# Layer 2 of a graph-attention kernel: both square roots of the norm ahead of the diagonals on ScalarE

## The chip, the cores and the metric

The kernel runs on one core of one Trainium2 chip. A core has five engines with a queue of instructions each: PE (TensorE, matrix products), DVE (VectorE), ACT (ScalarE), POOL (GpSimd, which here only issues gathers and scatters by index) and SP (SyncE, which issues plain DMAs). Each engine takes its own instructions in the order in which they were written, and waits on semaphores for the others. PE records stand in the profile as PE (the passes of a product) and PEld (weight loads). The metric is the device time of one execution in microseconds (us).

## What is computed

Two graph-attention layers on 10000 nodes with 768 features and about 170000 edges, then a residual and a layer norm. Cut to what matters (`gat_conv` is softmax attention over the edges that end in a node):

```python
h = gat_conv(x, edge_index, W1, a_src1, a_dst1, b1, HEADS, HID, True)     # 4 heads of 256
h = relu(layer_norm(h, g1, be1)) + (x @ Wr1 + br1)
h1 = h
h = gat_conv(h, edge_index, W2, a_src2, a_dst2, b2, 1, OUT_DIM, False)    # 1 head of 768
h = layer_norm(h, g2, be2)
h = h + (h1 @ Wr2 + br2)
x = _layernorm(x + h)
```

The change lies in layer 2: the attention sum of a row of table 2 over a node's edges, the norm with g2 and be2, the product of h1 with Wr2, and the last norm.

## The kernel before

A first stage computes table 1 (x times W1, with the attention terms) for all nodes and sorts the nodes by degree. `ordered_layer1` does layer 1 and writes table 2 (rows of 770 numbers) and h1. `ordered_layer2`, the function of this case, goes over 79 tiles of 128 nodes. Nodes of a tile have up to n edges; n is `SLOTS[t]` and grows over the tiles: 8, 9, 10, three of 11, three of 12, five of 13, six of 14, eight of 15, seven of 16, eight of 17, seven each of 18 and 19, six of 20, then four of 21 and so on up to 27, and a last tile of 41.

For edge slot k of a tile, POOL gathers 128 rows of table 2 into one place of a ring of 40 places (L393). The gather for a place waits until both readers of its old row are done. The weighted sum over the slots is split between two engines: DVE does columns 0 to 511 (`weigh`, L476, one instruction a slot, into `acc` in PSUM), PE does columns 512 to 767: ACT writes a diagonal matrix with the weights of slot k (L820), and PE multiplies it with the gathered rows and adds into `sum` (L821, two passes a slot in the records, after two passes of L814 for the bias). There are two buffers of four diagonals, so that the ninth diagonal has to wait until PE is done with the first four. PE also does the residual product of the next tile (L830 and L832, 36 passes).

All order is as written (`manual_schedule`). An iteration t of the loop at L842 does, for the tile before (`last`), the two norms and the store, and for tile t the attention sum:

- `stats = deviation(...)` (L855): DVE takes the statistics of `acc` and `sum` (L518, L520), ACT the square root (L522).
- `next(tail)` (L856): ACT writes the first n // 2 diagonals of tile t, PE multiplies them.
- `scaled` (L857; L531, L533, L534 on DVE), the residual is added (L858), `deviation` of the result (L859): DVE statistics, and the second square root on ACT.
- L861: the rest of the diagonals. L875: the residual product of tile t + 1 on PE.
- the loop over the slots (L888): DVE weighs slot k, POOL gets the gather of the place that this frees. After slot 1 comes `finish()` (L864): a reciprocal of the second square root on DVE (L865), L867, and on ACT the last scaling into `o` (L868). In the last three slots DVE and ACT make the weights of the next tile (`weights_of`: L804, L438 to L446 with an Exp on ACT, then L459 to L456).
- POOL scatters `o` to the output (L905). There is one buffer for `o`, so L868 waits until the scatter of the tile before has landed.

So ACT's order for a tile is: square root 1, diagonals 0 to n // 2 - 1, square root 2, the other diagonals, the last scaling, a table load, the Exp of the next tile, a table load.

Of the kernel before, what the change touches and what calls it, by code (L numbers as in the profile page):

```python
# [46 lines left out]
LEAD = 3  # L47
# [29 lines left out]
def gnn_kernel(ctx, tc, x, x_cols, src, dst, src_col, dst_col, W1, a_src1, a_dst1, b1, g1, be1, Wr1, br1,  # L77
# [7 lines left out]
    NT = -(-N // P)  # L85
# [4 lines left out]
    SLOTS = CAPS  # L90
# [301 lines left out]
    def gather(to, table, index, **more):  # L392
        nc.gpsimd.indirect_dma_start(out=to, out_offset=None, in_=table,  # L393
                                     in_offset=bass.IndirectOffsetOnAxis(ap=index, axis=0), **more)
# [152 lines left out]
    def load(s, w):  # L547
        nc.sync.dma_start(s[:, :, :w.shape[1]], w.rearrange("(k p) n -> p k n", p=P))
# [82 lines left out]
    SLOTS, FIRST = SLOTS[::-1], FIRST[::-1]  # L631
# [140 lines left out]
    def ordered_layer2():  # L772
        nonlocal ps_big
        with tc.tile_pool(name="b2", bufs=1) as pool, tc.tile_pool(name="small2", bufs=2) as small, \
                tc.tile_pool(name="ps_acc2", bufs=2, space=PSUM) as ps_acc, \
                tc.tile_pool(name="ps_q2", bufs=2, space=PSUM) as ps_big, tc.manual_schedule():
            ring = Ring(pool, table2, R2, RING2)
            ring.fetch(SLOTS[0])

            wr2, parts = w2[:, :, :C2], [wr1[:, k, :] for k in range(K0)]  # L780
            load(wr2, Wr2)
            b2_b, g2_b, be2_b = (spread(pool, v, n) for v, n in ((b2, "b2"), (g2, "g2"), (be2, "be2")))
            more = pool.tile([P, C2], F32, name="out")
            nc.scalar.dma_start(more, bass.AP(tensor=br2.tensor, offset=br2.offset, ap=[[0, P], [1, C2]]))
            nc.vector.tensor_add(be2_b, be2_b, more)
            brT = spread_br1(pool, "brT")
            more = pool.tile([P, C2], F32, name="out")
            nc.scalar.dma_start(more, shift.to_broadcast([P, C2]))
            nc.vector.tensor_add(b2_b, b2_b, more)

            def fetch_x(t):

                hT, xt = parts[t % 2], parts[2 + t % 2][:, :D0]
                nc.sync.dma_start(hT, h1_d[t])
                gather(xt, x[:, :], nodes(t))
                return hT.rearrange("p (k n) -> p k n", n=P), xt

            ones = pool.tile([1, P], F32, name="ones")
            nc.vector.memset(ones, 1.0)
            def weights_of(t):  # L800

                n = SLOTS[t]
                ad = small.tile([P, H2], F32, name="ad")
                nc.vector.tensor_add(ad, ring.slot(FIRST[t])[:, C2 + H2:], lift)  # L804
                e, _ = logits(small, ring, FIRST[t], FIRST[t] + n, ad, H2, C2)
                yield e
                normalised(small, e, H2, t)
                yield

            def sums(t, acc, e):  # L810


                n = SLOTS[t]
                nc.tensor.matmul(acc, ones, b2_b[0:1, ON_PE2:], start=True, stop=False)  # L814
                for k in range(n):
                    if k == n // 2:
                        yield
                    if k % G == 0:
                        diagonals = pool.tile([P, G, P], F32, name="diagonals", bufs=2)
                    nc.scalar.activation(diagonals[:, k % G, :], ident, AF.Copy, scale=e[:, k, :])  # L820
                    nc.tensor.matmul(acc, diagonals[:, k % G, :],  # L821
                                     ring.slot(FIRST[t] + k)[:, ON_PE2:C2], start=False, stop=(k == n - 1))

            def residual(t):

                hT, xt = ins.pop(t)
                r = ps_big.tile([P, 2 * BANK], F32, name="big")
                for c in range(0, C2, BANK):
                    d = min(C2, c + BANK)
                    nc.tensor.matmul(r[:, c:d], ident, xt[:, c:d], start=True, stop=False)  # L830
                    for j in range(K1):
                        nc.tensor.matmul(r[:, c:d], hT[:, j, :], wr2[:, j, c:d], start=False,  # L832
                                         stop=(j == K1 - 1))
                return r

            ins = {t: fetch_x(t) for t in range(min(2, NT))}
            ring.fetch(RING2)
            rs = {}
            last = None
            ready = []  # L840
            assert SLOTS[0] <= ring.size and NT > 1
            for t in range(NT + 1):  # L842
                live, tail = t < NT, iter(())
                n = SLOTS[t] if live else 0
                whole = live and n <= ring.size
                if whole and not ready:
                    ready = list(weights_of(t))
                if whole:
                    e = ready[0]
                    acc = ps_acc.tile([P, BANK], F32, name="acc")  # L850
                    sum_ = ps_acc.tile([P, BANK], F32, name="sum")[:, :C2 - ON_PE2]
                    tail = sums(t, sum_, e)
                if last:
                    h, r, means = last
                    stats = deviation(small, [a for m in means for a in pieces(m, C2 - ON_PE2)])  # L855
                    next(tail, None)  # L856
                    scaled(h, means, stats, g2_b, be2_b)  # L857
                    nc.vector.tensor_add(h, h, r[:, :C2])  # L858
                    mean, inv = deviation(small, pieces(h, C2 // 2))  # L859
                    o = pool.tile([P, C2], F32, name="out")  # L860
                for _ in tail:  # L861
                    pass

                def finish():  # L864
                    nc.vector.reciprocal(inv, inv)  # L865
                    less = small.tile([P, 1], F32, name="less")
                    nc.vector.scalar_tensor_tensor(less, mean, -1.0, inv, op0=OP.mult, op1=OP.mult)  # L867
                    nc.scalar.activation(o, h, AF.Identity, bias=less, scale=inv)  # L868

                if live:  # L870
                    if not t:
                        rs[0] = residual(0)
                        q = product(brT, wr2, C2)
                    elif t + 1 < NT:
                        rs[t + 1] = residual(t + 1)  # L875
                    r = rs.pop(t)
                    h_ = parts[4 + t % 2][:, :C2]
                    if not whole:
                        if last:
                            finish()  # L880
                        ad = small.tile([P, H2], F32, name="ad")
                        nc.vector.tensor_add(ad, ring.slot(FIRST[t])[:, C2 + H2:], lift)
                        attend_parts(small, ring, h_, h_, ad, b2_b, H2, DH2, t)
                    ready = []
                    ahead = iter(())
                    if whole and t + 1 < NT and SLOTS[t + 1] + LEAD <= ring.size:
                        ahead = weights_of(t + 1)
                    for k in range(n if whole else 0):  # L888
                        if k >= n - LEAD:
                            ready += itertools.islice(ahead, 1)  # L890
                        weigh(acc, ring.slot(FIRST[t] + k), e[:, k], ON_PE2, None if k else b2_b)
                        ring.fetch(FIRST[t] + k + 1 + ring.size)
                        if last and k == 1:
                            finish()
                        if not t and k == n - LEAD:
                            nc.vector.tensor_add(be2_b, be2_b, q[:, :C2])
                            rs[1] = residual(1)
                        if t + 2 < NT and k == n // 2:
                            ins[t + 2] = fetch_x(t + 2)
                    if t + 2 < NT and t + 2 not in ins:  # L900
                        ins[t + 2] = fetch_x(t + 2)
                elif last:
                    finish()
                if last:
                    nc.gpsimd.indirect_dma_start(  # L905
                        out=out, out_offset=bass.IndirectOffsetOnAxis(ap=nodes(t - 1), axis=0),
                        in_=o, in_offset=None, bounds_check=N - 1, oob_is_err=False)
                last = (h_, r, [acc, sum_] if whole else [h_]) if live else None
# [270 lines left out]
```

## Time and profile before

| | |
|---|---|
| median of 3 runs | 6021.35 us (6007.93 to 6030.65) |
| profiled execution | 6084.94 us; span of its instructions 6083.1 us |
| busy in the span | PE 4832.0 us, DVE 4447.5, ACT 3142.5, POOL 3401.9 |
| mean granted clock of PE | 0.890 |
| layer 2, first read of a finished `sum` to the end | 3751 to 6077 us |
| L820 diagonals on ACT | 1336 of 388 ns |
| L821 passes on PE | 2672 of 447 ns (they overlap) |
| L476 in layer 2, 512 columns, on DVE | 1258 of 755 ns |
| L868 last scaling on ACT | 78 of 1013 ns |
| L393 gathers of ring rows in layer 2, on POOL | 1356 of 965 ns |
| table loads on ACT in layer 2 | 77 before the square root, 77 before the Exp, 1283 ns each |

"Busy" is the time in which an engine executes; an engine that waits for a semaphore is idle. In the timeline, a line has the start, the length, the engine, the line of the program, what is written and read, the shapes, how many instructions the line merges, and in brackets the idle time of the engine before it with the engine that ended it ("issue" and "remote": the profile names none). PE's times are those of taking up a pass; its end is modelled.

### The profile page before, as it was taken

What the parts mean: (1) busy time and instruction counts of PE and PEld (TensorE: products, weight loads), DVE (VectorE), ACT (ScalarE), POOL (GpSimd) and SP (SyncE); (2) the same over time, 40 slices, a digit from 0 to 9 for tenths busy, and PEclk for the clock granted to TensorE, in tenths of its full rate; (3) what the DMA queues carried; (4) which work ended last, traced back from release to release, by engine and by line L of the source; (5) the groups of instructions that cost most, each with busy time, mean ns of one, the idle gap of its engine ahead of it and who ended that gap; (6) DMA issues with size and microseconds to landing.
All of it is one profiled execution on the core that took longest, in us unless ns stands there. A gap on an engine that the chain in (4) does not pass through costs nothing. (4 is left out here: it accounts for less than half of the span.)

```text
span 6083.1 us, 56565 instructions
## 1 busy us (share of the span) xinstructions
PE 4832.0 (79%) x14464; PEld 2808.5 (46%) x14464; DVE 4447.5 (73%) x7872; ACT 3142.5 (52%) x8061; POOL 3401.9 (56%) x3396
## 2 busy tenths in 40 slices
PE   8998896999999988888766546988877777777763
PEld 3443343555555554444433323555554555444442
DVE  5872433788999999999988883877666666666667
ACT  3433333678878888788877661333333333333321
POOL 3426444455556666556655525666666666666663
PEclk9999998999999999999888767999888888888876
DMA  4322326789999999999988847888887788887884
GB/s 141 121 86 67 88 87 214 271 297 321 331 327 326 339 340 331 329 324 335 332 314 316 296 166 256 293 292 293 287 269 261 264 277 280 278 281 267 273 272 152
DMA packets 438658, 1580.90 MB, mean 260 GB/s; under 512 B 102763, under 2 KB 106923, under 8 KB 438326
## 3 DMA queue, kind: packets, MB, share of 16 engines
q0 software_dynamic: 341344, 1400.80, 66.4%
q1 hardware_dynamic: 93168, 170.98, 8.5%
q10 hardware_dynamic: 3814, 5.39, 0.3%
q8 instruction: 122, 2.00, 0.1%
q14 instruction: 210, 1.72, 0.1%
HBM read 1431.10 MB, written 146.19 MB: 259 GB/s over the span
## 5 line engine op out<-in xcount | busy, mean ns | idle before, releaser
L393 POOL DMA_INDIRECT ring<-table,slots x2754 | 2622.5, 952 | 1826.0 <-issue 491.9
L476 DVE SCALAR_TENSOR_TENSOR acc<-ring,e,acc 128x256 f32<-128x256 f32 (+1 forms) x2606 | 1609.2, 618 | 189.7 <-PE acc L670 50.6
L465 ACT ACTIVATE ring<-ring,e 128x256 f32<-128x256 f32 x3536 | 1437.0, 505 | 0.0
L472 DVE TENSOR_TENSOR acc<-acc,ring 128x1024 f32<-128x1024 f32 x884 | 1089.1, 1232 | 85.7 <-ACT ring L465 9.4
L832 PE MATMUL big<-w,wr 128*128 128x512 f32 (+1 forms) x2528 | 878.7, 493 | 180.9 <-issue 177.8
L821 PE MATMUL sum<-ring,diagonals 128*128 128x256 f32 x2672 | 774.2, 447 | 258.4 <-issue 228.5
L161 PE MATMUL big<-w,xT 128*128 128x512 f32 x1896 | 834.6, 601 | 59.8 <-DMA xT<-in_x_cols_dram 38.0
L161 PE MATMUL big<-wr,xT 128*128 128x512 f32 x1896 | 866.2, 615 | 17.6 <-ACT xT L543 17.6
L820 ACT ACTIVATE diagonals<-ident,e 128x128 f32<-128x128 f32 x1336 | 424.0, 388 | 846.5 <-PE sum L821 668.7
L161 PE MATMUL big<-w,hT 128*128 128x512 f32 (+1 forms) x2528 | 833.3, 487 | 1.2 <-ACT hT L543 1.2
L821 PEld LDWEIGHTS sum<-ring,diagonals 128*128 128x128 f32 x2672 | 597.2, 227 | 451.2 <-issue 333.9
L832 PEld LDWEIGHTS big<-w,wr 128*128 128x128 f32 x2528 | 484.5, 192 | 527.0 <-issue 495.4
L161 PEld LDWEIGHTS big<-w,hT 128*128 128x128 f32 x2528 | 478.8, 189 | 376.0 <-issue 341.4
L161 PEld LDWEIGHTS big<-w,xT 128*128 128x128 f32 x1896 | 363.5, 193 | 527.5 <-issue 503.0
L161 PEld LDWEIGHTS big<-wr,xT 128*128 128x128 f32 x1896 | 370.6, 199 | 458.3 <-issue 440.5
L670 PE MATMUL acc<-ring,diagonals 128*128 128x256 f32 x1248 | 336.0, 430 | 284.4 <-ACT diagonals L665 251.8
L670 PEld LDWEIGHTS acc<-ring,diagonals 128*128 128x128 f32 x1248 | 269.5, 219 | 345.3 <-ACT diagonals L665 266.2
L618 DVE TENSOR_TENSOR scr<-big,as_b 128x1024 f32<-128x1024 f32 x79 | 96.7, 1224 | 451.8 <-ACT row L615 428.9
L623 POOL TENSOR_TENSOR row<-row,none 128x1024 f32<-128x1024 f32 x79 | 187.0, 2367 | 341.9 <-ACT row L615 341.3
L522 ACT ACTIVATE sd<-mv,eps 128x1 f32<-128x1 f32 x237 | 69.2, 292 | 576.6 <-issue 253.0
L446 ACT ACT_TABLE_LOAD x155 | 198.9, 1283 | 315.6 <-DVE e L445 226.5
L621 ACT ACTIVATE scr<-scr 128x256 f32<-128x256 f32 x632 | 253.5, 402 | 122.2 <-DVE scr L618 117.0
(171 smaller groups left out, 3973.3 us busy)
## 6 DMA issues: line engine op xcount, KB each, us to landing
ring<-table,slots POOLq DMA_INDIRECT x2754
table<-row SPq DMA_DIRECT2D x79, 516.0 KB
h_d<-hT SPq DMA_DIRECT2D x79, 512.0 KB
wr<-h_d SPq DMA_DIRECT2D x79, 512.0 KB
xT<-in_x_cols_dram SPq DMA_DIRECT2D x79, 384.0 KB
w<-in_W_dram SPq DMA_DIRECT2D x6, 512.0 KB
w<-in_W_dram SPq DMA_DIRECT2D x1, 3072.0 KB
wr<-in_Wr_dram SPq DMA_DIRECT2D x1, 3072.0 KB
```

The source lines that it names most:

```text
L161: nc.tensor.matmul(p[:, c:e], aT[:, j, :], w[:, j, c:e], start=(j == 0), stop=(j == k - 1))
L393: nc.gpsimd.indirect_dma_start(out=to, out_offset=None, in_=table, in_offset=bass.IndirectOffsetOnAxis(ap=index, axis=0), **more)
L446: nc.scalar.activation(e, e, AF.Exp)
L465: nc.scalar.activation(row[:, s], row[:, s], AF.Copy, scale=e[:, h:h + 1])
L472: nc.vector.tensor_add(acc[:, :c], acc[:, :c], row[:, :c])
L476: nc.vector.scalar_tensor_tensor(acc[:, s], row[:, s], e[:, h:h + 1], (acc if first is None else first)[:, s], op0=OP.mult, op1=OP.add)
L621: nc.scalar.activation(m[:, s], m[:, s], AF.Copy, accum_out=row[:, C1 + i * H1 + h:C1 + i * H1 + h + 1])
L623: nc.gpsimd.tensor_add(row[:, :C1], row[:, :C1], b1_b)
L670: nc.tensor.matmul(acc[:, c:d], diagonals[:, k * H1 + i, :], ring.slot(FIRST[t] + k)[:, c:d], start=(k == 0 and c % BANK == 0), stop=(k == ...
L820: nc.scalar.activation(diagonals[:, k % G, :], ident, AF.Copy, scale=e[:, k, :])
L821: nc.tensor.matmul(acc, diagonals[:, k % G, :], ring.slot(FIRST[t] + k)[:, ON_PE2:C2], start=False, stop=(k == n - 1))
L832: nc.tensor.matmul(r[:, c:d], hT[:, j, :], wr2[:, j, c:d], start=False, stop=(j == K1 - 1))
```

## The change

Within an iteration, both square roots now come ahead of the diagonals on ACT; the first half of the diagonals follows the second statistics; the second half, and the residual product behind it, follow `finish()` after slot 1.

```diff
-            assert SLOTS[0] <= ring.size and NT > 1
+            assert LEAD <= SLOTS[0] <= ring.size and NT > 1
...
                     stats = deviation(small, [a for m in means for a in pieces(m, C2 - ON_PE2)])
-                    next(tail, None)
                     scaled(h, means, stats, g2_b, be2_b)
                     nc.vector.tensor_add(h, h, r[:, :C2])
                     mean, inv = deviation(small, pieces(h, C2 // 2))
                     o = pool.tile([P, C2], F32, name="out")
-                for _ in tail:
-                    pass
+                    next(tail, None)
+                else:
+                    for _ in tail:
+                        pass
...
                         q = product(brT, wr2, C2)
-                    elif t + 1 < NT:
-                        rs[t + 1] = residual(t + 1)
...
                         if last and k == 1:
                             finish()
+                            for _ in tail:
+                                pass
+                            if t + 1 < NT:
+                                rs[t + 1] = residual(t + 1)
...
+                    if t + 1 < NT and t + 1 not in rs:
+                        rs[t + 1] = residual(t + 1)
```

In the built program the instructions on PE, DVE, POOL and SP stand in the same order as before, one by one; only ACT's order differs. For a tile it is now: square root 1, square root 2, diagonals 0 to n // 2 - 1, the last scaling, the other diagonals, a table load, the Exp of the next tile, a table load.

## The prediction

> **What bounds the kernel now.** I read the waits of layer 2 first (engine, line, what it waited for; total us, times, longest), then the stretches by n, then the timeline of single tiles.
>
> ```profile
> ACT diagonals L820 <- PE sum L821: 668.7, 158, 15.9
> POOL ring L393 <- PE sum L821: 328.2, 200, 8.0
> DVE sd L865 <- ACT sd L522: 146.2, 29, 11.0
> ```
>
> The third line is what the change takes away. The timeline gives it a place: only tiles with n of 18 or more have it. Their first half is nine or more diagonals, the buffers hold eight, so square root 2 stands behind a diagonal that waits for PE. With n up to 17 it comes 5.4 us after DVE's read of the finished `sum`, every time.
>
> Whether these 146 us lie on the path is a matter of what paces a tile. The stretches (PE, PEld, DVE, ACT, POOL busy, clock, DMA share, GB/s) run from one read of `sum` to another, and hold the 8 tiles of n = 15, 8 of 17, 7 of 18 and 7 of 19:
>
> ```profile
> 4151.60:4351.97 200.37, 170.67 (x545) 111.10 (x544) 148.76 (x316) 71.22 (x168) 134.05 (x137) 0.91 0.86 292
> 4557.82:4800.33 242.51, 188.64 (x576) 121.26 (x577) 161.80 (x331) 76.67 (x184) 143.34 (x150) 0.83 0.78 261
> 4800.33:5011.33 211.00, 163.52 (x517) 108.46 (x516) 146.24 (x298) 68.26 (x168) 133.75 (x138) 0.85 0.82 275
> 5011.33:5228.66 217.33, 164.85 (x530) 110.23 (x530) 152.07 (x307) 69.97 (x175) 141.40 (x148) 0.84 0.84 283
> ```
>
> A tile takes 25.05, 30.31, 30.14 and 31.05 us. POOL issues n + 2 transfers a tile (n rows, a row of x, the scatter), one every 1.25 us (0.95 busy, 0.30 to the next), and DMA moves about 315 GB/s while it does. That is 21.25, 23.75, 25.00 and 26.25 us. The rest, 3.8, 6.6, 5.1 and 4.8 us, is mostly a pause of POOL. By the same count n = 14 has 3.4, n = 16 has 6.9, n = 20 has 5.8, and the 15 tiles from 21 to 27 have 6.6 on average. So POOL's issues and one pause a tile make the period. A tile with n = 19:
>
> ```profile
> 5200.61 3.50 PE L821 MATMUL sum<-ring,diagonals 128*128 128x256 f32 x15
> 5207.22 1.02 POOL L905 DMA_INDIRECT out_dram<-out,order  x1 [0.30 <-issue]
> 5211.61 0.40 ACT L820 ACTIVATE diagonals<-ident,e 128x128 f32<-128x128 f32 x1 [10.55 <-remote]
> 5211.72 0.98 POOL L393 DMA_INDIRECT ring<-table,slots  x1 [3.48 <-remote]
> 5211.92 0.28 ACT L522 ACTIVATE sd<-mv,eps 128x1 f32<-128x1 f32 x1
> ```
>
> PE takes up slots 0 to 7 by 5204.1, but ACT and POOL, which both need slot 0 done, go on at 5211.6. In between POOL has stopped for lack of free places; DMA falls from a share of 0.93 (5200 to 5208) to 0.39 (5210.6 to 5211.7), and as it runs dry the waits end. The tiles that I looked at show the same: PE's completions come late while gathers keep DMA full, and together when they stop. Why, the profile doesn't say.
>
> DVE is not in this ring: it sits idle for 7.83 us before 5212.23 and POOL issues at full pace after. PE's sum starts where the residual ends (5200.06), not when a diagonal comes.
>
> **The change part by part.** The order on PE, DVE, POOL and SP stays, so the residual is not moved in PE's own queue; no instruction, table load or DMA is added. Three things move on ACT.
>
> *Square root 2 ahead of the diagonals.* It takes 0.29 us, and DVE's reciprocal no longer waits: minus 146.2 us of DVE idle time. Behind that wait are the weights of slots 2 to n - 1, and behind slot 2 one gather. That costs POOL a second pause in about two thirds of the tiles with n of 18 or more:
>
> ```profile
> 5242.59 0.97 POOL L393 DMA_INDIRECT ring<-table,slots  x1 [4.52 <-PE sum L821]
> 5243.87 0.95 POOL L393 DMA_INDIRECT ring<-table,slots  x1 [0.30 <-issue]
> 5247.59 0.95 POOL L393 DMA_INDIRECT ring<-table,slots  x1 [2.77 <-PE sum L821]
> ```
>
> The third gather needs the place of slot 2. PE is named, but ACT's ninth diagonal shows PE done with slots 0 to 3 by 5244.92, while DVE weighs slot 2 from 5246.10 to 5246.87. I count some 25 such tiles at about 2 us: 50 us of POOL time that go.
>
> What comes instead is read from n = 16 and 17, where the wait does not exist today: there the one pause is 6 to 7 us, the tile 6.9 and 6.6 us over POOL's issues, and DVE waits up to 9.4 us for the end of the sum. With the wait gone, n of 18 and more has the order of n = 17. If the tiles take its 6.7 us, they change by (6.7 - 5.1) x 7 + (6.7 - 4.8) x 7 + (6.7 - 5.8) x 6 + (6.7 - 6.6) x 15 = 31 us slower. If they take the 3.6 of n = 14 and 15: (1.5 + 1.2) x 7 + 2.2 x 6 + 3.0 x 15 = 77 us faster. I take the first, as the nearer row in n and in order of work.
>
> *First half behind square root 2.* Its start moves from 0.9 to 5.7 us after the read of `sum`. PE is then in the residual (36 passes, 11.7 us). In tiles up to 17 the sum starts 7 to 12 us after that read, so the residual covers the delay by 1.5 us or more. From 18 on it starts 2.4 us after the read, but the read itself comes some 4 us earlier once DVE doesn't wait. Cost 0; if that cover fails, up to 4.8 - 1.5 = 3.3 us in 35 tiles, 116 us.
>
> One rule speaks against this part. The Trainium skill (TensorE: Matmul & The Clock Gate, "Part 1: The HAM clock gate") says that after an idle window of about 3.4 us the array runs at half rate. The rows show such phases already: 15 passes in 3.50 us at 5200.61, and 5 in 2.50 us at 5212.07 with a granted clock of 0.50. By the rule a sum that starts late would take twice its passes' time; by the rows, PE works on the residual meanwhile and nothing is added.
>
> *The last scaling ahead of the second half.* It leaves the way of the Exp (1.01 us sooner) and enters the way of the diagonals. In ACT's queue the diagonals, the table load and the Exp stand behind it, and PE's sum and DVE's L459 wait for those. It waits for slot 1's reciprocal, 7 us after the read of `sum`, and for the scatter of the tile before, as `o` has one buffer; today it comes so late that the second wait is 17.1 us in all. The scatter is issued just before POOL's pause. By the DMA shares it lands 3.4 to 4.5 us after its issue. For the tile of n = 13 (read of `sum` at 3900.65) the scatter is issued at 3912.65, lands at 3916.0 to 3917.2, and the scaling ends 1.01 later, at 3917.0 to 3918.2. Diagonals 6 and 7 are written at 3906 today, the eighth and later ones from 3915.71, the Exp at 3919.51. Seven diagonals (2.0 us) and a table load (1.3) behind the scaling put the Exp at 3920.3 to 3921.5, and slots 6 and 7 on PE behind the pause. So 0.8 to 2.0 us later in the 27 tiles with n up to 15, 22 to 54 us, mean 38. POOL's pause may hide it all, and the sum's end moves out by as much as today lies between n = 15 and 16, where the pause doubles. Between 0 and 54 I take 22, a little over half the mean. With n of 16 and 17 the scatter comes 5 to 10 us ahead of the ninth diagonal: 0. From 18 on it is 1.0 us behind that diagonal, in the pause's shadow: 0, at most 35 us.
>
> Sum against the profiled execution: 6084.9 + 31 + 22 = 6138, 0.9% more. It stands 1.06% over the median of the runs; by the same share, 6021 becomes 6074.
>
> **The rivals.**
> *The second pause goes and the first stays short* (faster). For it: the 50 us above, and the 3 us pause that every other tile from 18 on already has. Against it: n = 16 and 17. Price 50 to 77 us, 0.8 to 1.3%: 5944 to 5971. It decides if DVE's earlier read also lets PE take up eight slots before DMA runs dry.
> *Nothing moves.* DMA must run dry once a tile whatever ACT does, and what one pause loses the other gains: 0, give or take 25 us. For it: the time over POOL's issues is 5 to 7 us from n = 16 to 27, with one pause or two. 5996 to 6046.
> *More of the small tiles tip over* (slower still). If n = 14 and 15 go from 3.4 and 3.8 to 6.7: 3.3 x 6 + 2.9 x 8 = 43 us, with the 31: 74 us, 6095; with the 35 us of late diagonals, 6130.
> *That DVE's wait is on the path whole*, minus 146 us, 5875: against it stands POOL, which runs on through that wait.
>
> **How the numbers follow.** 0.5%, 30 us, is about what a measurement of this kernel can tell from no change. Slower, as forecast or with more tiles tipped: 0.52. Nothing moves: 0.24. Faster: 0.24, of which 0.02 below 5940. The likeliest case's own range is 6052 to 6130. Leaving out the ends of both sides, 5955 to 6130 should hold 8 in 10.
>
> **What would show it.** In the profile after, L865's 146 us on L522 must vanish; if it stays, the change does not do what it says. Right: the stretches of n = 18 and 19 at 31.7 and 32.9 us a tile, one POOL pause of 6 to 7 us in each, L868 waiting for the scatter's DMA, the Exp 1 to 2 us later in tiles up to 15. Wrong: stretches of n = 18 and 19 under 29.5 us, or a first `sum` pass of a tile that starts late with ACT as its releaser.

## The result and the profile after

The changed kernel takes 6066.4 us (5 runs, 6061.54 to 6074.03), the kernel before 6025.61 us in the same comparison (5 runs, 6007.93 to 6035.92). The ratio is 1.0071, interval 1.0050 to 1.0091: slower by 0.7%, as forecast in sign; forecast were 6074 us and 0.9%.

One caution comes first. The profiled execution of after took 6074.03 us and is one of these five. That of before took 6084.94 us and lies above all of its five. In a later comparison the same program took 6066 to 6085 us, and in three others 5703 to 5720. So the two profiles may not come from alike chips (for the result no chip is noted): they are compared by stage, not by their totals. And the traces of this level hold fewer semaphore events (updates of a semaphore, with their times), 39286 for before and 42229 for after, than a trace of the same program at 5705 us (74590, the run of before again below). What ended a wait is told from these events, so the names behind the arrows are less sure here, and "issue" and "remote" more frequent; the idle times themselves come from the instructions.

Some of the waits of layer 2 after the change (engine, line, what it waited for: total us, times, longest):

```profile
PEld big L832 <- issue: 548.9, 1441, 3.3
POOL ring L393 <- PE sum L821: 235.5, 192, 7.0
DVE st L518 <- remote: 214.0, 29, 13.1
ACT diagonals L820 <- PE sum L821: 188.6, 111, 10.6
ACT out L869 <- DMA out_dram<-out,order: 146.9, 23, 9.2
DVE st L518 <- PE big L832: 133.9, 15, 14.6
PEld sum L821 <- ACT diagonals L820: 101.1, 56, 5.9
...
DVE sd L866 <- ACT sd L522: 0.4, 1, 0.4
```

The last line is the wait that the change takes away: 146.2 us became 0.4. Three others grew, which stood so before:

```profile
DVE st L518 <- remote: 66.7, 9, 11.0
DVE st L518 <- PE big L832: 39.9, 8, 6.7
ACT out L868 <- DMA out_dram<-out,order: 17.1, 3, 16.1
PEld sum L821 <- ACT diagonals L820: 14.8, 3, 8.4
```

DVE now waits 348 us for the end of the sum (L518, both lines), where the same lines of before gave 66.7 and 39.9. The last scaling waits 146.9 us for the scatter, before 17.1. PE's weight loads for the sum wait 101.1 us for a diagonal, before 14.8. The stretch of n = 16 before, which the prediction does not show:

```profile
4351.97:4557.82 205.85, 168.29 (x513) 109.07 (x512) 136.31 (x285) 64.26 (x154) 127.07 (x133) 0.86 0.81 271
```

The stretches of n = 15 to 19 after the change, cut as before:

```profile
4151.40:4347.97 196.57, 170.00 (x547) 109.12 (x546) 148.75 (x316) 70.87 (x168) 133.21 (x137) 0.92 0.86 296
4347.97:4537.53 189.56, 158.55 (x499) 104.83 (x498) 136.36 (x285) 65.01 (x154) 124.32 (x129) 0.88 0.84 286
4537.53:4784.12 246.59, 200.77 (x594) 127.14 (x593) 161.50 (x331) 76.77 (x184) 150.23 (x157) 0.84 0.79 268
4784.12:5002.33 218.21, 175.14 (x517) 112.43 (x518) 146.57 (x298) 68.92 (x168) 133.02 (x140) 0.85 0.81 271
5002.33:5227.40 225.07, 179.54 (x534) 115.54 (x534) 152.01 (x306) 71.00 (x175) 142.08 (x148) 0.83 0.82 276
```

By 8, 7, 8, 7 and 7 tiles that is 24.57, 27.08, 30.82, 31.17 and 32.15 us, before 25.05, 29.41, 30.31, 30.14 and 31.05. From n = 13 to 16 no tile loses, and those of n = 16 gain 2.3 us each; n = 17 loses 0.5, n = 18 and 19 lose 1.0 and 1.1 us each. The result's 41 us can't be found in this pair of profiles: the 15 us of n = 18 and 19 are outweighed by the 16 us of n = 16, and from the first read of a finished `sum` to the end the profile after is the shorter one, 2321.4 against 2332.0 us. A tile with n = 18:

```profile
4909.02 0.43 DVE L518 BATCH_NORM_STATS2 st<-sum 128x6 f32<-128x256 f32 x1 [9.47 <-PE big L832]
...
4914.35 0.29 ACT L522 ACTIVATE sd<-mv,eps 128x1 f32<-128x1 f32 x1 [4.29 <-DVE mv L520]
4914.55 2.43 ACT L820 ACTIVATE diagonals<-ident,e 128x128 f32<-128x128 f32 x8
4914.98 10.38 PE L821 MATMUL sum<-ring,diagonals 128*128 128x256 f32 x36 [1.92 <-ACT diagonals L820]
...
4916.48 0.97 POOL L393 DMA_INDIRECT ring<-table,slots  x1 [4.43 <-PE sum L821]
...
4939.92 0.94 POOL L393 DMA_INDIRECT ring<-table,slots  x1 [2.46 <-remote]
```

DVE waits 9.47 us for the sum, ACT's first diagonal comes 5.5 us after the read, and PE, done with the residual, starts on it 1.92 us late. POOL pauses twice, 4.43 and 2.46 us. Summed over the timelines of all 14 tiles with n = 18 and 19, POOL's pauses (idle for more than 0.6 us) were 22 of 73.4 us in all before and are 31 of 87.4 us now: 14 us more, nearly all that these tiles lose. The last scaling waits for the scatter in one of the 14, for 0.6 us. The sum's last pass is taken up by 4925.2, yet DVE reads it only at 4940.43: PE's completions come late, as in the profile before.

### The profile page after: what moved, and what is told of

The parts are those of the page before. It is cut to its first block, busy times and chain, and to the rows that moved or that the text cites. A ratio compares the mean times of both kernels' runs of the same rounds, so it can differ in the third digit from the quotient of the medians.

```text
span 6072.1 us, 56539 instructions
## 1 busy us (share of the span) xinstructions
PE 4866.0 (80%) x14464; PEld 2817.1 (46%) x14464; DVE 4447.8 (73%) x7872; ACT 3146.2 (52%) x8061; POOL 3397.7 (56%) x3396
## 5 line engine op out<-in xcount | busy, mean ns | idle before, releaser
L832 PE MATMUL big<-w,wr 128*128 128x512 f32 (+1 forms) x2528 | 927.1, 508 | 208.0 <-issue 203.9
L821 PE MATMUL sum<-ring,diagonals 128*128 128x256 f32 x2672 | 753.5, 443 | 220.0 <-issue 141.3
L832 PEld LDWEIGHTS big<-w,wr 128*128 128x128 f32 x2528 | 500.2, 199 | 597.8 <-issue 565.5
L820 ACT ACTIVATE diagonals<-ident,e 128x128 f32<-128x128 f32 x1336 | 420.0, 388 | 314.3 <-PE sum L821 188.6
```

The lines of the kernel that those rows point to most:

```text
L821: nc.tensor.matmul(acc, diagonals[:, k % G, :], ring.slot(FIRST[t] + k)[:, ON_PE2:C2], start=False, stop=(k == n - 1))
```

## The experiments

Theory A is the prediction: tiles with n of 18 and more take the long pause, and the last scaling costs some in the small ones. Theory B, from the rows above: PE's late start on the first diagonal is the loss. Theory C: the last scaling's wait for the scatter, with the second half of the diagonals behind it, is the loss. D and E came up later, with the extra load. Kernels of one comparison share its chip and its runs of before:

| comparison | before, median us | kernel | ratio to before (interval) |
|---|---|---|---|
| 1 | 5711.56 | before again | 0.9994 (0.9985 to 1.0004) |
| 1 | | square root only | 1.0003 (0.9994 to 1.0012) |
| 1 | | last scaling only | 1.0178 (1.0164 to 1.0192) |
| 1 | | first half of at most 8 | 0.9999 (0.9990 to 1.0008) |
| 2 | 5713.84 | the change again | 1.0155 (1.0139 to 1.0170) |
| 2 | | the change, two output buffers | 0.9958 (0.9945 to 0.9972) |
| 2 | | before, two output buffers | 0.9961 (0.9948 to 0.9975) |
| 3 | 6071.65 | the change, early scatter | 1.0102 (1.0085 to 1.0118) |
| 3 | | before, extra load | 1.0004 (0.9994 to 1.0013) |
| 3 | | the change, extra load | 1.0038 (1.0024 to 1.0052) |
| 4 | 5712.39 | square root only, again | 0.9995 (0.9986 to 1.0004) |
| 4 | | the change, two output buffers, again | 0.9957 (0.9944 to 0.9971) |

**Before again.** No edit.

> The kernel before once more, for the spread of one kernel against itself and for a second profile: the profiled execution of before stands 1% over the median of its runs. Every theory expects a ratio of 1.000, give or take 0.002, and a profiled execution nearer to 6025 us. If the stretches of n = 18 to 20 come out at 30, 31 and 33 us a tile again, those of the first profile can be compared with the changed kernel's 31.2, 32.2 and 33.5; if they come out lower, they can't.

The ratio is 1, but the level is 5712 us, 5% under that of the result. The profile differs just where the prediction had its mechanism. The waits of layer 2:

```profile
ACT out L868 <- DMA out_dram<-out,order: 569.2, 66, 17.4
...
PEld big L832 <- issue: 299.8, 1248, 0.2
...
ACT diagonals L820 <- PE sum L821: 124.5, 131, 4.7
...
POOL ring L393 <- PE sum L821: 78.3, 251, 1.5
...
DVE sd L865 <- ACT sd L522: 3.7, 4, 1.7
```

PE's weight loads never stand for more than 0.2 us in the residual, ACT waits 124.5 us for PE where it was 668.7, and POOL waits for PE 1.5 us at the longest, was 8.0. A tile takes 21.7 us at n = 15 and 24.5 at n = 17, POOL's issues (21.25 and 23.75) and little more. So the pause belongs to the conditions of the first profile, not to the program. Periods in us a tile, from the times at which DVE reads the finished sum:

| profile (comparison) | n=13 | 14 | 15 | 16 | 17 | 18 | 19 | 20 | 21-27 |
|---|---|---|---|---|---|---|---|---|---|
| before (first) | 22.1 | 23.4 | 25.1 | 29.4 | 30.3 | 30.1 | 31.1 | 33.3 | 37.8 |
| after (result) | 21.8 | 23.1 | 24.6 | 27.1 | 30.8 | 31.2 | 32.2 | 33.5 | 37.6 |
| before, extra load (3) | 22.1 | 23.3 | 25.7 | 28.9 | 31.1 | 29.1 | 31.4 | 33.3 | 38.0 |
| after, extra load (3) | 22.0 | 23.5 | 25.1 | 28.7 | 30.9 | 31.9 | 32.5 | 33.1 | 37.7 |
| before again (1) | 19.0 | 19.9 | 21.7 | 22.6 | 24.5 | 25.5 | 26.6 | 28.5 | 31.7 |
| after again (2) | 21.9 | 22.9 | 23.9 | 24.3 | 25.5 | 26.2 | 27.9 | 27.8 | 31.7 |
| after, two buffers (2) | 18.1 | 20.3 | 21.5 | 23.5 | 24.7 | 26.0 | 27.3 | 28.6 | 31.7 |

**One part at a time.**

```diff
 square root only (of before):
-                    next(tail, None)
                     scaled(h, means, stats, g2_b, be2_b)
...
                     o = pool.tile([P, C2], F32, name="out")
+                    next(tail, None)
                 for _ in tail:
 last scaling only (of after):
+                    next(tail, None)
                     scaled(h, means, stats, g2_b, be2_b)
...
                     o = pool.tile([P, C2], F32, name="out")
-                    next(tail, None)
 first half of at most 8 (of before):
-                    if k == n // 2:
+                    if k == min(n // 2, 2 * G):
```

> Only the second square root is moved ahead of the first half of the diagonals; the last scaling stays behind the second half. Theory A (the prediction): tiles with n of 18 and more take the long pause once DVE reads the sum early, 31 us slower, and the last scaling costs another 22 in the change: this run at 1.005. Theory B (from the profile after): the whole loss is PE's sum that now starts on the first diagonal, 6.0 us after the read of the sum, with PE idle for 1 to 2.3 us before it in some 25 tiles; the place of the last scaling costs nothing: this run at 1.007 (41 us), as the change itself. Theory C: the loss is the last scaling's wait for the scatter: 0.995 to 1.000.

> Only the last scaling is moved ahead of the second half; the second square root stays behind the first half. Theory A: 22 us slower, 1.004. Theory B: nothing, 1.000, give or take 0.002. Theory C: 41 us slower, 1.007. DVE's wait for the second square root stays in all three.

> The kernel before with a first half of at most 8 diagonals instead of n // 2, so that the second square root no longer stands behind a ninth diagonal, while the first diagonals stay at 0.9 us after the read of the sum. DVE's 146 us of waiting must vanish in every theory. Theory A: the tiles with n of 18 and more take the long pause as n = 17 does, 31 us slower, 1.005. Theory B: without the late first half the loss is gone, and what the wait was worth shows: 0.992 to 1.000.

At this level of before the square root's place costs nothing and the last scaling's place costs 1.78%. That is more than any theory gave (1.007 at most); A and B fall here, C stands in sign. DVE's wait for square root 2 is 3.7 us in the run of before again, so there is nothing for a first half of 8 to gain, and it gains nothing.

**The change again, and a second output buffer.** The edit, the same for before and after: `bufs=2` on the three tiles named "out".

```diff
-                    o = pool.tile([P, C2], F32, name="out")
+                    o = pool.tile([P, C2], F32, name="out", bufs=2)
```

> The changed kernel itself, as an anchor beside the runs of before, which took 5712 us in the last comparison and 6026 us in the one of the result: the execution of one and the same program depends on the chip. Theory C (the last scaling waits for the scatter with the second half of the diagonals behind it): on a chip where before takes 5712 us, as the kernel with only the last scaling moved, 1.016 to 1.020; where before takes 6026 us, 1.007. Theory B (PE's sum starts late, behind the second square root): 1.003 to 1.007 on both.

> The changed kernel with two buffers for the output tile, so that the last scaling doesn't wait for the scatter of the tile before; nothing else is changed. Theory C: the loss goes, 0.998 to 1.002 of before, and the waits of the last scaling for the scatter's DMA (147 us in the profile after) fall under 20 us. Theory B: the ratio stays that of the changed kernel. Theory A (the prediction): two fifths of the loss go (22 of 53 us), on a chip with 1.007 that leaves 1.004.

> The kernel before with two buffers for the output tile. Where before takes 5712 us its last scaling waits 569 us for the scatter, with a table load and the Exp of the next tile behind it, and DVE waits 161 us for that Exp. If these waits are on the path, up to 2% faster (0.98 to 0.995); if POOL's issues set the pace there (n + 2 of 1.25 us make 21.25 us of the 21.7 us of a tile with n = 15), no change, 0.997 to 1.001. Where before takes 6026 us its last scaling waits 17 us in all: 1.000.

The change costs 1.55% at this level, and with two buffers nothing is left of it: 0.9958 against 0.9961 for before with two buffers. Theory C is shown for this level. Both also beat the kernel before by 0.4%, which lies between the two cases expected for before with two buffers (0.98 to 0.995, or 0.997 to 1.001), and of the kernels run at this level they are the quickest. The timelines of two tiles with n = 15 show the mechanism. First the change again, the wait in all of layer 2, then ACT's and PE's rows:

```profile
ACT out L869 <- DMA out_dram<-out,order: 372.5, 57, 12.1
```

```profile
4126.18 2.14 ACT L820 ACTIVATE diagonals<-ident,e 128x128 f32<-128x128 f32 x7
4138.27 1.03 ACT L869 ACTIVATE out<-wr,less,sd 128x768 f32<-128x768 f32 x1 [9.96 <-DMA out_dram<-out,order]
4139.20 2.68 ACT L820 ACTIVATE diagonals<-ident,e 128x128 f32<-128x128 f32 x8
```

```profile
4129.94 3.29 PE L821 MATMUL sum<-ring,diagonals 128*128 128x256 f32 x14
4139.64 6.50 PE L821 MATMUL sum<-ring,diagonals 128*128 128x256 f32 x16 [6.41 <-ACT diagonals L820]
```

and POOL's scatter in the same tile:

```profile
4131.44 1.02 POOL L910 DMA_INDIRECT out_dram<-out,order  x1 [0.30 <-issue]
```

The scatter of the tile before is issued at 4131.44. The scaling is released at 4138.27, 6.8 us later, after a wait of 9.96. The eight diagonals of the second half stand behind it, and PE, done with slots 0 to 6 at 4133.2, stands still for 6.41 us. Then with two buffers:

```profile
ACT out L869 <- DMA out_dram<-out,order: 1.6, 2, 1.2
```

```profile
4113.07 2.14 ACT L820 ACTIVATE diagonals<-ident,e 128x128 f32<-128x128 f32 x7
4115.12 1.01 ACT L869 ACTIVATE out<-wr,less,sd 128x768 f32<-128x768 f32 x1
4116.03 0.39 ACT L820 ACTIVATE diagonals<-ident,e 128x128 f32<-128x128 f32 x1
```

The scaling follows the first half at once, and in all of layer 2 it waits 1.6 us for the scatter, where the change again has 372.5. The table places the loss: from n = 12 to 17 the tiles of after again take 80 us more than those of before again, of 95.6 us between the two spans.

**Early scatter and extra load.**

```diff
 early scatter (of after): the scatter moves from the end of the tile into its loop
+                        if last and k == n // 2:
+                            scatter()
...
 extra load (of before and of after), into a tile that nobody reads:
+                        if k == n // 2:
+                            nc.sync.dma_start(pool.tile([P, D0], F32, name="extra"), x[min(t * P, N - P):min(t * P, N - P) + P, :])
```

> The changed kernel with one buffer for the output tile, but POOL issues the scatter right after the gather that follows slot n // 2, not behind the last gather of the tile. It is then issued some n / 2 gathers, 8 to 10 us, earlier, and lands before the last scaling of the next tile asks for the buffer. Theory C (the wait for the scatter is the whole loss): the loss goes as with two buffers, 0.994 to 1.001. Theory B (PE's late start): it stays at 1.007 to 1.016. If POOL now waits for the last scaling, a new wait, it stays slower, 1.005 or more.

> The kernel before with one more plain load of 393 KB a tile in layer 2, which nobody reads. It tests what makes the two comparisons of before differ (6026 and 5712 us). POOL's pace asks DMA for 17 rows of 394 KB and 512 KB of h1 in 21.25 us at n = 15, 339 GB/s; DMA moved 335 there in the run that took 5712 us, and 300 to 318 in stretches without a pause in the first profile. Theory D (a few per cent less from DMA make gathers fall behind until the ring runs full, and pauses come with it): 5% more to move gives the pauses and the times of the first profile, 25 us a tile at n = 15 and 30 at n = 17, 1.04 to 1.055 of before. Theory E (DMA's extra work is simply added): 0.393 MB by 330 GB/s is 1.2 us a tile, 92 us in all, 1.016. If this comparison runs where before takes 6026 us, 1.01 to 1.03.

> The changed kernel with the same extra load. To be read against the run of before with that load: by theory D the kernel before then has the pauses already and the change adds little, after by before 1.003 to 1.010, as in the result; by theory E the wait for the scatter grows with DMA's queue, 1.015 or more.

This comparison ran at 6072 us. 393 KB more per tile, 5% at n = 15, cost the kernel before nothing (1.0004). Neither D's nor E's price appears, nor the 1.01 to 1.03 expected for this level; that DMA has room where POOL pauses would explain it, but is not shown by itself. D's question, whether more bytes bring the pauses on where there are none, has no run at 5712 us. With the extra load the change costs 0.34% (6094.89 against 6074.90), and its profile says where: from the extra load in before to that in after the tiles of n = 18 and 19 take 27 us more, those of 12 to 17 take 4 us less. POOL's pauses in the tiles of n = 18 and 19 go from 25 of 74.3 us to 34 of 98.9 us, again nearly the whole loss there. The stretches of n = 18 and 19, first before with the load, then after with it:

```profile
4803.64:5007.40 203.76, 163.02 (x508) 108.39 (x509) 146.28 (x298) 68.26 (x168) 130.52 (x135) 0.84 0.85 289
5007.40:5227.37 219.97, 166.79 (x537) 111.70 (x536) 152.00 (x306) 70.19 (x175) 142.83 (x148) 0.84 0.85 293
```

```profile
4802.57:5025.84 223.27, 175.73 (x518) 111.13 (x519) 146.35 (x297) 68.64 (x168) 133.29 (x140) 0.84 0.83 278
5025.84:5253.14 227.30, 182.73 (x530) 116.58 (x530) 152.09 (x306) 71.01 (x175) 140.09 (x146) 0.81 0.85 282
```

The early scatter does not cure the change at this level, though the wait nearly goes:

```profile
ACT out L874 <- DMA out_dram<-out,order: 17.6, 10, 5.7
```

It is 146.9 us in the profile after and 159.4 in that with the load. The run alone does not rule theory C out here, as it has its own side effect: the scatter now stands ahead of half a tile's gathers on POOL, and the tiles from n = 18 on take 32.6 to 39.2 us, more than those of after. What speaks against C at this level is the place: in the tiles of n = 18 and 19, where both pairs of profiles lose, the last scaling waits for the scatter for 0.6 us in all after the change, and not at all with the load.

**Once more.** The square root alone and the two buffers were run again, in the hope of a comparison at the higher level.

> Only the second square root ahead of the first half, again; the comparison tells which kind of chip it ran on by the time of before. Where before takes about 5712 us: 1.000, as measured. Where before takes 6026 to 6072 us, theory A (the first step of the prediction) expects the loss here, in the tiles with n of 18 and 19 (31.2 to 31.9 and 32.2 to 32.5 us a tile in both profiles of the changed kernel, 29.1 to 30.1 and 31.1 to 31.4 in both of before): 1.003 to 1.007. Theory C (the scatter alone) expects 0.998 to 1.001 there too.

> The changed kernel with two buffers for the output tile, again. Where before takes about 5712 us: 0.996, as measured. Where before takes 6026 to 6072 us: by theory A the loss in the tiles with n of 18 and 19 stays, 1.003 to 1.007; by theory C it goes, 0.996 to 1.001. The second square root comes early in both kernels of this call, so only the last scaling and its buffer differ.

It came out at 5712 us, and both ratios repeat. For the higher level the two parts are therefore not told apart by a run, and the change alone has there no second measurement: beside the result's 0.7% stands only the 0.34% of the pair with the extra load.

## Why the prediction was right, and where it was not

*The wait that goes.* Right: L865's 146.2 us became 0.4, and the time did not fall by them. The rival that put that wait wholly on the path is out.

*Tiles with n of 18 and more take the order of n = 17.* Right in place and size for n = 18 and 19 at the level it was read from, wrong in the step that led there. Forecast for n = 18 and 19 were 31.7 and 32.9 us; measured 31.17 and 32.15 in the result's profile, 31.9 and 32.5 with the extra load. The step gave 24 us for these two; they cost 15 and 27 us in the two pairs of profiles. For n = 20 and above it gave 7 us; nothing was lost there (1.1 and -1.4 us at n = 20; -2.5 and -4.9 us from 21 to 27). The step that failed is POOL's second pause: 50 us of it were to go with the wait, and it did not go. In the 35 tiles from 18 on POOL pauses 82 times instead of 63, for 232.6 us instead of 215.5 (with the load 85 instead of 65, 236.8 instead of 216.7). One pause of 6 to 7 us was forecast for n = 18 and 19; there are about two, of 6.2 us together (7.1 with the load). The wait that takes the place of L865's is the one named, DVE's for the end of the sum.

*Cost of the first half behind square root 2.* This step was wrong as stated. "The residual covers the delay" fails from n = 18 on: in 20 of the 35 tiles the sum starts at 6.0 us after the read, behind the first diagonal, and PE stands 0.2 to 2.3 us before it. The prediction named this row as a sign that it is wrong. Its reading that the sum starts 2.4 us after the read before the change holds for about half of the tiles: of the 14 with n = 18 and 19, 8 start at 1.6 to 3.3 us and 6 at 9.2 to 13.3, four of these after a stop of PE as well. Before the first pass PE stands 14.7 us in all in these 14 tiles, before 7.9 (with the load 12.2 and 7.7); over all 35 tiles it stands no longer than before (29.7 us, before 34.0). What the late start costs at 6026 to 6072 us no run separates from the pause. At 5712 us it costs nothing: with the square root alone moved, PE's loads wait 286.5 us for diagonals, in the run of before again 286.9, and the ratio is 1.0003 and 0.9995. The clock hardly moved: 0.85 and 0.83 granted in the stretches of n = 18 and 19, before 0.85 and 0.84. The rows decided rightly. What the Trainium skill (TensorE: Matmul & The Clock Gate, "Part 1: The HAM clock gate") says of an idle window of about 3.4 us was not tested by these starts, as PE stood at most 2.3 us before them.

*The last scaling ahead of the second half.* The mechanism is right (a buffer, a scatter's landing, diagonals and the Exp behind it), the term was mis-sized, and in both directions. At the level of the profiles, 22 us were forecast for n up to 15, with the Exp 0.8 to 2.0 us later. Measured: the Exp comes 21.1 us after the read of the sum at n = 15, before 21.6; 19.7 at n = 14, before 20.0; and the stretches of n = 13 to 16 are no longer than before. There the second half waits for PE's late completions anyway (668.7 us of ACT's waiting before, 188.6 after), and the wait for the scatter fits into that one. The prediction had this as its lower end ("POOL's pause may hide it all") and took 22. At 5712 us nothing hides it: the term is 80 us from n = 12 to 17, of which 19 are in n = 16 and 17, where it was put at 0, and the landing takes 4.5 to 6.8 us in the two tiles looked at, where 3.4 to 4.5 were read from DMA's shares. So that 31 + 22 = 53 came near the result's 41 us was in part luck. In the profiles of that level the tiles of the first term lose 14 us (21 with the load) and the second term is nil, and the rest of the 41 us is not placed; the second term was a guess between ends that two kinds of conditions realise.

*The rivals.* "Nothing moves", give or take 25 us, is outside the result's interval (30 to 55 us); the 20 us of the pair with the extra load would lie inside it. "Faster" would have needed the first pause to stay short, and at n = 18 it did not. "More of the small tiles tip over" did not happen at the higher level (n = 14 and 15 went from 23.4 and 25.1 to 23.1 and 24.6 us); at the lower one these tiles slowed by 3.0 and 2.2 us, by the scatter and not by the rival's pause.

*What stays open.* Why PE's completions come late at 6026 to 6072 us and not at 5712. That it is the chip is likely, as each comparison ran on one chip (6, 11 and 4 at 5712 us, 7 at 6072), but no run shows it. Nor do the runs show whether it has to do with the semaphore events, of which the traces of that level hold little more than half. How the 0.7% splits there between PE's late start and the pause stays open too, and where the part of it lies that the pair of profiles does not show.

## What to carry to other kernels

An instruction that waits for a DMA, moved ahead of the work that feeds another engine, can put the DMA's landing on that engine's path; look whether the buffer it writes has a second copy before moving it. Here the second copy costs one argument and undoes the loss at 5712 us (1.0155 became 0.9958). And read more than one profile: a cost found in one, such as the pause that set every tile here, can be missing from the next run of the same program, and the size of a change with it (1.0071 and 1.0155).

## What the runs showed of the hardware that was not expected

- One program takes 5712, 6026 or 6072 us (medians of the comparisons), steady within 0.5% in each, the profiled execution of 6084.94 us apart. Most of the difference lies in layer 2, whose first read of a sum is at 3751 us in the first profile and at 3718 in the run of before again.
- At the higher level PE's weight loads in the residual wait up to 3.3 us each for nothing that the profile shows (484.9 us before), at the lower one 0.2 us (299.8).
- 393 KB more to load in each of 78 tiles costs 0.04% (interval -0.06% to 0.13%) at 6072 us.
- With one output buffer the tiles of the change alternate at 5712 us: 26.0 and 19.4 us by turns near n = 14 and 15. The scatter is issued 10.8 us after the read of the sum in the long tile at 4120.66 and 5.4 and 7.0 us after it in the short ones on either side.
